# Four vector jobs moved in the steady step of a four-layer graph network

## The chip, the cores and the metric

The kernel runs on one core of one Trainium2 chip. The metric is device time in microseconds (us) of one execution. Times of runs are medians; the profile comes from one profiled execution of its own. The engines are named as in the profile: PE (TensorE matmuls), PEld (its weight loads), DVE (VectorE), ACT (ScalarE), POOL (GpSimd), SP (the queue that issues most transfers).

## What is computed

The input is x of 128 graphs x 64 nodes x 512 features, all float32, and a 64 x 64 matrix adj for each graph. Four layers follow each other; each adds its result to x and normalizes over the features. Cut to what matters:

```
H = (adj != 0);  Dn = 1 / (H @ adj[0]);  Be = 1 / column sums of H
conv(x, W, b) = Dn * (H @ (Be * (H.T @ (x @ W.T)))) + b
layer 0: h = layernorm(relu(conv(x, W1, b1))) * gamma + beta     # 512 -> 1024
         x = norm(x + conv(h, W2, b2) + x)                       # 1024 -> 512
layer 1: A = exp(leaky(8 * tanh((s_i + s_j) / 8))) * adj, rows normalized, times row sums of adj;  s = (x @ w) @ a
         x = norm(x + A @ x @ w)
layer 2: y = relu(adj @ (x @ W1) + b1); y = relu(adj @ (y @ W2) + b2)
         x = norm(x + adj @ (y @ W3) + b3)
layer 3: attention with 8 heads of 64; softmax(q k' / 8) * 0.33 + 0.33 * adj + 0.33 * exp(-adj), times v
         x = norm(x + heads @ W_out + b_out)
```

The mask that comes with the input is all true here; the kernel computes with it nonetheless.

## The kernel before

**Tiling.** Two graphs make a pair of 128 rows, four pairs a group (`G = 4`, 512 rows). The 128 graphs make 16 groups (`NGRP`), numbered q. `xg` holds a group's x and is changed in place by all layers.

**Products with weights.** Every product of a group with a 512 x 512 weight is a two by two block product with seven instead of eight block products (the scheme of Strassen and Winograd). The left side is a `Left`: its tile `aT_...` holds the transposed operand in four quadrants, and its method `sums` (lines 483 to 491) makes four sums of quadrants on DVE: s1, s2 and s4 in a tile `s_...`, s3 in place. The function `multiply` (line 514) issues the seven block products in the order B11, T1, T2, B21, T3, B22, T4, each through `product` (line 496). B11, T2, T3 and T4 go into one PSUM accumulator (`a_...`), T1 and B22 into a second (`b_...`), B21 into a third (`c_...`). Between them the accumulators are copied as they stand: u1 after B11, u5 after T1, u2 after T2 (function `snap`, line 521). With a residual the copy is an addition on DVE (line 526), without one it is a copy on ACT (line 524). T2 adds into the accumulator that u1 reads, so T2 has to wait for u1; T3 waits for u2 in the same way. Outputs are formed on DVE from an accumulator and a copy (lines 544, 548, 552), the last one on ACT or DVE (lines 555, 557). A block product is 8 passes of PE (16 in the product with W2, whose left side has two halves). In the profile a float32 matmul shows as two passes.

**Products with a graph's matrix** are 64 x 64 matmuls on quarters of PE (`graph_T`, line 448; profile names `gt_l`, `gt_l0h`, `gth`): 128 passes each, evacuated by ACT copies (line 466).

**Buffers.** PSUM has four accumulators (`ps_acc`) and four buffers for the small products (`ps_gt`). Weights come through a ring of 20 tiles (`RING`) by the SP queue, in the order of use.

**Order.** Three groups are in work at once: in a step, part `a` is layers 0 and 1 of group q, part `b` layer 2 and the first part of layer 3 of group q - 1, part `t` the end of layer 3 of group q - 2. Each is a generator (`first_half`, `second_half`) that stops at named points, and a list `order` (line 1205) written by hand says in which order the pieces are emitted; steps 2 to 15 are the steady ones. A scheduler then places each engine's instructions: among those that it reckons ready it takes the one that was emitted first. `tc.issue_after` holds instructions of an engine back until a named instruction of the same engine has been placed. The helper `behind(key)` (line 471) does this with an instruction that was put in the dictionary `last_add`. In the finished program each engine runs its list from front to back.

**Names around the change**, with the line where each stands:

- `left.sums()` of layer 2 (line 987), in `second_half`; its operand comes from `gt_l<-atc,x`.
- `doubled` and `constant` (lines 787 and 793): x becomes 2x + b2, and then x + cs * bw, where cs is a column scaling of the graph and bw a constant row. Both are emitted behind the last-but-one output of the first half block `l0w10` (lines 700 to 703).
- the eight sums of the two halves of the hidden layer (lines 723 and 724; names `s_l0h`, `aT_l0h`), between `c2a` and `c2b`.
- `gb3` (line 1002): four additions of a bias to x of group b; after it `prepare_masks` (lines 654 to 666; names `neg`, `m`, `adt`). Both stand behind the last-but-one output of the product `l2b`.
- `attend` (line 1172): the product of the probabilities with v, in two halves (duos) of two PSUM tiles each (`pv`), and the two scaled ACT copies of each duo into `aT_oT` (line 1195). The `osum` piece is the sums of that operand.

The end of the steady list, before the change:

```
    order = """
        t.v1 a.c1 t.v b.gt t.soft a.w1a1 a.w1a t.soft2 a.resid b.l2a1 b.l2a a.w1b1 t.ptp a.w1b t.pv a.lnh t.osum
        b.l2b1 a.c2a b.l2b a.c2b b.gb3 load a.w21 b.gh a.w2 rows b.l2c1 b.l2c2 a.ss b.l2c t.o1 a.den t.o2 a.c3 b.agg t.o
```

Of the kernel before, what the change touches and what calls it, by code (L numbers as in the profile page):

```python
# [8 lines left out]
FP = mybir.dt.float32  # L9
# [5 lines left out]
P = 128  # L15
# [7 lines left out]
Q = 256  # L23
# [18 lines left out]
def kernel(  # L42
# [31 lines left out]
    NGRP = NPAIR // G  # L74
# [6 lines left out]
    sp = ctx.enter_context(tc.tile_pool(name="sp", bufs=3))  # L81
# [54 lines left out]
    ten, vec, act = Engine(nc.tensor, PE), Engine(nc.vector, DVE), Engine(nc.scalar, ACT)  # L136
# [288 lines left out]
    def row2(t, c0):  # L425

        return t[:, c0 : c0 + Q].unsqueeze(1).to_broadcast([P, 2, Q])
# [38 lines left out]
            act.copy(o[:, :, :, g, :], ps[g])  # L466


    last_add = {}

    def behind(key):
        return tc.issue_after(last_add[key]) if key in last_add else nullcontext()

    class Left:
# [6 lines left out]
        def quad(self, m, k):  # L481
            return self.t[:, 2 * k : 2 * k + 2, m * Q : (m + 1) * Q]

        def sums(self):
            s = sp.tile([P, 3, 2, Q], FP, name=f"s_{self.key}", tag="s")
            s1, s2, s4 = (s[:, n] for n in range(3))
            s3 = self.quad(1, 0)
            vec.tensor_add(s1, s3, self.quad(1, 1))
            vec.tensor_sub(s2, s1, self.quad(0, 0))
            vec.tensor_sub(s3, self.quad(0, 0), s3)  # L490
            vec.tensor_sub(s4, self.quad(0, 1), s2)
            self.left = {
                B11: self.quad(0, 0), B21: self.quad(0, 1), B22: s4, T4: self.quad(1, 1),
                T1: s1, T2: s2, T3: s3,
            }
            return self
# [19 lines left out]
    def multiply(lefts, wt_q, dst, key, flipped=False, res=None, stops=(3,)):  # L516


        acc = [ps_acc.tile([P, 2, Q], FP, name=f"{n}_{key}", tag="acc") for n in "ab"]

        def snap(ps, m, n, what):
            t = work.tile([P, 2, Q], FP, name=f"{what}_{key}", tag="w")
            if res is None:
                act.copy(t, ps)
            else:
                vec.tensor_add(t, ps, res(m, n))  # L526
            return t

        pa, pc = acc
        product(pa, lefts, wt_q, B11, True, False, flipped)  # L530
        s1 = snap(pa, 0, 0, "u1")
        if 1 in stops:
            yield
        product(pc, lefts, wt_q, T1, True, False, flipped)
        s5 = snap(pc, 1, 1, "u5")
        if 2 in stops:
            yield
        product(pa, lefts, wt_q, T2, False, False, flipped)
        s2 = snap(pa, 0, 1, "u2")
        if 3 in stops:  # L540
            yield
        pb = ps_acc.tile([P, 2, Q], FP, name=f"c_{key}", tag="acc")
        product(pb, lefts, wt_q, B21, True, True, flipped)
        vec.tensor_add(dst(0, 0), pb, s1)
        if 4 in stops:
            yield
        product(pa, lefts, wt_q, T3, False, False, flipped)
        vec.tensor_add(dst(1, 1), pa, s5)  # L548
        if 5 in stops:
            yield  # L550
        product(pc, lefts, wt_q, B22, False, True, flipped)
        last_add[key] = vec.tensor_add(dst(0, 1), pc, s2).ins  # L552
        product(pa, lefts, wt_q, T4, False, True, flipped)
        if res is None:
            act.copy(dst(1, 0), pa)
        else:
            vec.tensor_add(dst(1, 0), pa, res(1, 0))
# [9 lines left out]
    def turned(t):  # L567

        return lambda m, n: t[:, 2 * n : 2 * n + 2, m * Q : (m + 1) * Q]
# [100 lines left out]
    def first_half(g):  # L670
        q, xg = g["q"], g["x"]
        pair = lambda p: xg[:, p, :]

        left = Left(f"l0_{q}")
# [5 lines left out]
        for n in range(2):  # L680
            for i, _ in enumerate(multiply(
                [left], (w_1[n], q),
                lambda m, k: h[m][:, :, n * D + k * Q : n * D + (k + 1) * Q],
                f"l0w1{n}_{q}",
                res=lambda m, k: row2(b1_bc, n * D + k * Q),
                stops=((2, 4), (2, 3))[n] if q == 1 else (3,),
            )):
                yield f"w1{'ab'[n]}{i + 1}"
            yield "w1" + "ab"[n]

            if n == 0:
                st = small.tile([P, G, 2, 6], FP, name=f"sth_{q}", tag="sth", bufs=2)
            with behind(f"l0w1{n}_{q}"):
                for m in range(2):
                    hn = h[m][:, :, n * D : (n + 1) * D]
                    act.activation(hn, hn, AF.Relu)  # L696
                    for p in range(2):
                        vec.bn_stats(st[:, 2 * m + p, n, :], hn[:, p, :])
            if n == 0:
                if q > 1:  # L700
                    with behind(f"l0w10_{q}"):
                        doubled(g)
                        constant(g)
                yield "resid"
        for m in range(2):
            mv = small.tile([P, 2, 2], FP, name=f"mvh_{q}_{m}", tag="mvh")
# [8 lines left out]
        lefts = [Left(f"l0h{u}_{q}") for u in range(2)]  # L715
        for duo in range(2):
# [3 lines left out]
                )  # L720
            if duo == 0:
                yield "c2a"
        for left in lefts:
            left.sums()
        yield "c2b"
        gen = multiply(lefts, (w_2, q), nat(xg), f"l0w2_{q}", res=nat(xg))
        next(gen)
# [4 lines left out]
        s4 = small.tile([P, G], FP, name=f"s4_{q}", tag="s4")  # L732
# [14 lines left out]
        t = grp.tile([P, G, C], FP, name=f"t_{q}", tag="t", bufs=1)  # L747
# [16 lines left out]
        left = Left(f"l1_{q}")  # L764
# [26 lines left out]
    def constant(g):  # L791
        for p in range(G):
            vec.scalar_tensor_tensor(
                g["x"][:, p, :], bw_bc, g["cs"][:, p : p + 1], g["x"][:, p, :], ALU.mult, ALU.add
            )
# [184 lines left out]
    def second_half(g):  # L980
        q, xg = g["q"], g["x"]
        pair = lambda p: xg[:, p, :]

        left = Left(f"l2_{q}")
        for duo in range(2):
            graph_T(pair, g["atc"], left.t, duo, f"l2_{q}")
        left.sums()
        yield "gt"
        h1 = Left(f"h1_{q}")
        for _ in multiply([left], (w_g[0], q), turned(h1.t), f"l2a_{q}", flipped=True):  # L990
            yield "l2a1"
# [5 lines left out]
        for _ in multiply([h1], (w_g[1], q), nat(g2), f"l2b_{q}"):  # L997
            yield "l2b1"
        yield "l2b"
        with behind(f"l2b_{q}"):  # L1000
            for p in range(G):
                vec.tensor_add(xg[:, p, :], xg[:, p, :], gb3_bc)
            prepare_masks(g)
# [4 lines left out]
        for c2 in range(2):  # L1008
            ps = [ps_gt.tile([P, 2, G, C], FP, name=f"gth2_{q}_{c2}_{h}", tag="gt") for h in range(2)]
            for c in range(2):  # L1010
                for p in range(G):
                    for f in range(2):
                        for h in range(2):
                            rows, c0 = slice(h * C, (h + 1) * C), (2 * c2 + c) * P + f * C
# [18 lines left out]
        for duo in range(2):  # L1033
            ps = [ps_gt.tile([P, D], FP, name=f"agg_{q}_{duo}_{p}", tag="gt") for p in range(2)]
            for h in range(2):
                for p in range(2):
                    rows = slice(p * C, (p + 1) * C)
# [11 lines left out]
        left = Left(f"xT_{q}")  # L1049

        for duo in range(2):
            ps = [ps_gt.tile([P, KD, 2, C], FP, name=f"xtp_{q}_{duo}_{h}", tag="gt") for h in range(2)]
            for c in range(KD):
                for p in range(2):
                    for h in range(2):
                        rows = slice(h * C, (h + 1) * C)
# [20 lines left out]
        v = big.tile([P, G, D], FP, name=f"v_{q}", tag="big")  # L1077
# [10 lines left out]
        pts = [turn_probs(g, duo, probs[duo]) for duo in range(2)]  # L1088
        yield "ptp"
        left = Left(f"oT_{q}")  # L1090
        for duo in range(2):
            attend(g, duo, pts[duo], v, left)
        yield "pv"
        left.sums()
        yield "osum"
        for n, _ in enumerate(multiply([left], (w_o, q), nat(xg), f"wo_{q}", res=nat(xg), stops=(1, 3))):
# [75 lines left out]
            pts.append(pt)  # L1172
        return pts

    def attend(g, duo, pts, v, left):

        q = g["q"]

        ps = [ps_acc.tile([P, 4, 2, C], FP, name=f"pv_{q}_{duo}_{gg}", tag="acc") for gg in range(2)]
        for hc in range(4):  # L1180
            for p in range(2):
                for h2 in range(2):
                    hd = 2 * hc + h2
                    for gg in range(2):
                        rows = slice(gg * C, (gg + 1) * C)
                        ten.matmul(
                            ps[gg][h2 * C : (h2 + 1) * C, hc, p, :],
                            v[rows, 2 * duo + p, hd * C : (hd + 1) * C],
                            pts[p][rows, h2 * 4 + hc, :],
                            start=True,  # L1190
                            stop=True,
                        )
        o4 = left.t[:, :, duo * Q : (duo + 1) * Q].rearrange("p c (a g i) -> p c a g i", a=2, g=2)
        for gg in range(2):
            act.mul(o4[:, :, :, gg, :], ps[gg], LA)  # L1195
# [7 lines left out]
        a0.c31 constant1 a1.w1a keep3 a1.resid a0.l12 a1.w1b1 a0.l13 a1.w1b2 b0.gt a1.w1b  # L1203
    """.split()
    order = """
        t.v1 a.c1 t.v b.gt t.soft a.w1a1 a.w1a t.soft2 a.resid b.l2a1 b.l2a a.w1b1 t.ptp a.w1b t.pv a.lnh t.osum
        b.l2b1 a.c2a b.l2b a.c2b b.gb3 load a.w21 b.gh a.w2 rows b.l2c1 b.l2c2 a.ss b.l2c t.o1 a.den t.o2 a.c3 b.agg t.o
        a.p1 b.xT a.p2 b.q1 b.q t.ln3 b.k1 prep b.k b.dots
    """.split()

# [5 lines left out]
    todo = []  # L1216
    for what in start:
        who, dot, name = what.partition(".")
# [7 lines left out]
    for step in range(1, NGRP + 2):  # L1226
        for what in order if step > 1 else step_1:
            who, dot, name = what.partition(".")
            key = (who, step - lag[who], name) if dot else (what, step + 1, None)
# [126 lines left out]
```

## Time and profile before

| | |
|---|---|
| median of 3 runs | 2805.87 us (2805.82 to 2807.02) |
| profiled execution | 2804.13 us |
| its span | 2802.3 us |
| PE busy | 2769.3 us, 99% of the span |
| PEld busy | 2362.0 us, 84% |
| DVE busy | 2003.7 us, 72% |
| ACT busy | 818.2 us, 29% |
| granted clock of PE, mean | 0.999 |
| a steady step | 171.8 us |

The span runs from the first to the last instruction; the profiled execution's own time is 1.8 us longer than its span. In the timeline each row gives the start in us from the span's start, the duration in us, the engine, the source line, the operation, the tiles (out<-in), the shapes, how many instructions were merged, and in brackets the idle time before the row with the instruction that ended it. A busy PE is not a PE at its peak, since matmuls overlap; the distance between the starts of two rows says more than the duration of a row. All times of single instructions given here are from one steady step, which begins about 1183 us into the span, and from the start of the next.

### The profile page before, as it was taken

The numbers are of one execution on the slowest core, as the hardware profiler recorded it, in microseconds if no ns is written. First come the engines' busy times: TensorE is split into PE (matmuls) and PEld (weight loads), VectorE is DVE, ScalarE is ACT, GpSimd is POOL, SyncE is SP. The second block draws the span as 40 slices with busy tenths as digits, with TensorE's granted clock in tenths as the row PEclk, the third lists the DMA queues.
The fourth block names the chain that finished last, engine by engine and source line by source line (L and its number), as shares of the span: only waits on it lengthen the run. The fifth ranks groups of instructions, "written<-read, shape, count | busy, mean of one in ns | idle before, by whom it ended". The sixth has DMA issues, their size and how long they took to land.

```text
span 2802.3 us, 67764 instructions
## 1 busy us (share of the span) xinstructions
PE 2769.3 (99%) x28862; PEld 2362.0 (84%) x28862; DVE 2003.7 (72%) x3861; ACT 818.2 (29%) x1467; POOL 38.1 (1%) x72
## 2 busy tenths in 40 slices
PE   9999999999999999999999999999999999999998
PEld 7878888888888888888888888888888888888877
DVE  6768677676776767767677776767767677676756
ACT  3223323232232322322233232232323223232222
POOL 2000000000000000000000000000000000000000
PEclk9999999999999999999999999999999999999999
DMA  8444454454544545445454454545545454454541
GB/s 259 165 127 148 130 158 140 139 162 131 165 129 136 163 129 166 127 142 163 133 158 130 142 160 128 162 129 150 152 133 162 130 158 135 132 162 129 147 118 64
DMA packets 309660, 405.94 MB, mean 145 GB/s; under 512 B 57424, under 2 KB 184944, under 8 KB 309360
## 3 DMA queue, kind: packets, MB, share of 16 engines
q1 hardware_dynamic: 304384, 385.84, 46.5%
q0 software_dynamic: 4976, 15.76, 1.5%
q8 instruction: 229, 3.75, 0.5%
q14 instruction: 71, 0.58, 0.1%
HBM read 370.57 MB, written 30.93 MB: 143 GB/s over the span
## 4 chain that ended last, share of the span: by engine, by line
PE 86%; DVE 8%; ACT 1%; issue 0%; DVEq 0%
PE a_l0w L509 13%; PE b_l0w L509 7%; PE a_l2b L509 4%; PE a_q L509 4%; PE a_k L509 4%; PE a_v L509 4%; PE c_l0w L509 4%; PE a_l2a L509 4%; PE a_l1w L509 4%; PE gt_l L458 3%; PE a_wo L509 3%; PE a_l2c L509 2%; PE gt_l0h L458 2%; PE b_l1w L509 2%; PE b_v L509 2%; PE b_l2b L509 2%
## 5 line engine op out<-in xcount | busy, mean ns | idle before, releaser
L509 PE MATMUL a_l0w<-w2w,aT_l0h 128*128 128x256 f32 x720 | 164.3, 381 | 0.0
L440 DVE BATCH_NORM_STATS2 st_l<-x 128x6 f32<-128x512 f32 x248 | 160.2, 674 | 0.1
L509 PEld LDWEIGHTS a_l0w<-w2w,aT_l0h 128*128 128x128 f32 x720 | 135.6, 190 | 18.8
L696 ACT ACTIVATE h<-h 128x1024 f32<-128x1024 f32 x58 | 61.3, 1057 | 216.6 <-DVE h L552 195.0
L444 DVE TENSOR_SCALAR x<-x,mv_l,rs_l 128x512 f32<-128x512 f32 x248 | 120.1, 542 | 1.8
L466 ACT COPY aT_l<-gt_l 128x512 f32<-128x512 f32 x176 | 90.5, 600 | 71.1 <-PE gt_l L458 71.0
L509 PE MATMUL b_l0w<-w2w,s_l0h 128*128 128x256 f32 x480 | 108.5, 379 | 0.0
L509 PEld LDWEIGHTS b_l0w<-w2w,s_l0h 128*128 128x128 f32 x480 | 90.1, 190 | 13.5
L1023 ACT ACTIVATE aT_h<-gth,gb_col 128x256 f32<-128x256 f32 x128 | 48.4, 489 | 159.0 <-PE gth L1015 159.0
L431 ACT ACTIVATE rs_l<-mv_l,eps_t 128x4 f32<-128x4 f32 (+1 forms) x63 | 18.8, 298 | 258.1 <-DVE mv_l L441 256.8
L509 PE MATMUL a_l2b<-gwbw,aT_h 128*128 128x256 f32 x360 | 86.9, 384 | 4.7 <-ACT aT_oT L1195 4.7
L509 PE MATMUL a_l2a<-aT_l,gwaw 128*128 128x256 f32 x360 | 86.6, 383 | 1.0 <-ACT aT_l L466 1.0
L509 PE MATMUL a_q<-aT_xT,wqw 128*128 128x256 f32 x360 | 86.6, 383 | 0.2 <-ACT aT_xT L1062 0.2
L509 PE MATMUL a_v<-wvw,aT_xT 128*128 128x256 f32 x360 | 86.6, 383 | 0.0
L509 PE MATMUL a_l2c<-gwcw,aT_h 128*128 128x256 f32 x360 | 85.3, 380 | 0.6 <-DVE g L548 0.6
L509 PE MATMUL a_wo<-wow,aT_oT 128*128 128x256 f32 x360 | 85.3, 380 | 0.0
L509 PE MATMUL a_l1w<-ww,aT_l 128*128 128x256 f32 x360 | 85.1, 379 | 0.0
L509 PE MATMUL a_k<-aT_xT,wkw 128*128 128x256 f32 x360 | 85.0, 379 | 0.0
L509 PE MATMUL a_l0w<-w1aw,aT_l 128*128 128x256 f32 x336 | 82.3, 388 | 0.0
L509 PE MATMUL a_l0w<-w1bw,aT_l 128*128 128x256 f32 x336 | 81.7, 379 | 0.0
L526 DVE TENSOR_TENSOR u_l0w<-a_l0w,b_bc 128x512 f32<-128x512 f32 x56 | 38.5, 688 | 59.8 <-PE a_l0w L509 59.8
L509 PEld LDWEIGHTS a_l2b<-gwbw,aT_h 128*128 128x128 f32 x360 | 67.1, 190 | 15.2 <-ACT aT_oT L1195 6.6
(503 smaller groups left out, 6464.5 us busy)
## 6 DMA issues: line engine op xcount, KB each, us to landing
w2w<-w2k SPq DMA_DIRECT2D x210, 256.0 KB, 2.7
x<-in_x_dram SPq DMA_DIRECT2D x15, 1024.0 KB, 6.3
w1aw<-w1ak SPq DMA_DIRECT2D x60, 256.0 KB, 2.7
w1bw<-w1bk SPq DMA_DIRECT2D x60, 256.0 KB, 2.7
ww<-wk SPq DMA_DIRECT2D x60, 256.0 KB, 2.7
gwaw<-gwak SPq DMA_DIRECT2D x60, 256.0 KB, 3.7
gwbw<-gwbk SPq DMA_DIRECT2D x60, 256.0 KB, 2.7
gwcw<-gwck SPq DMA_DIRECT2D x60, 256.0 KB, 2.7
```

The lines of the kernel that those rows point to most:

```text
L431: act.activation(rs[:, at], mv[:, at, 1], AF.Sqrt, bias=eps_t)
L440: vec.bn_stats(st, xg[:, p, :])
L444: vec.tensor_scalar(xg[:, p, :], xg[:, p, :], mv[:, p, 0:1], rs[:, p : p + 1], ALU.subtract, ALU.mult)
L458: ten.matmul(ps[g][f * C : (f + 1) * C, c, p, :], src(2 * duo + p)[rows, c0 : c0 + C], mat[rows, 2 * duo + p, :], start=True, stop=True,)
L466: act.copy(o[:, :, :, g, :], ps[g])
L509: ten.matmul(acc[:, blk, :], lhsT, rhs, start=(first and blk == 0 and i == 0), stop=(last and i == n_k - 1), skip_group_check=True,)
L526: vec.tensor_add(t, ps, res(m, n))
L696: act.activation(hn, hn, AF.Relu)
L1023: act.activation(o[:, :, h, :], ps[h][:, c].rearrange("p (d a) i -> p d (a i)", d=2), AF.Relu, bias=gb2_col[:, k : k + 1],)
```

## The change

Four things move; no arithmetic is added or removed.

1. `Left.sums` can make a part of its sums. In the steady steps the sums of layer 2 of group q are emitted behind the copy u2 of the next group's first half block (`l0w10`). The first and last group keep the old place.
2. `constant` moves from behind `l0w10` to behind the last-but-one output of `l2b`, ahead of the sums of the hidden layer; these sums are emitted quadrant sum by quadrant sum for both halves.
3. `gb3` and the masks move from behind that output of `l2b` to behind the last of the hidden layer's sums.
4. The ACT copies of the second duo of the value product are emitted behind u1 of `l2b`, and the sums of that operand after `b.l2b1`.

To make this possible, `snap` records its instructions in `last_add`. The core of the diff:

```diff
-        def sums(self):
-            s = sp.tile([P, 3, 2, Q], FP, name=f"s_{self.key}", tag="s")
-            s1, s2, s4 = (s[:, n] for n in range(3))
+        def sums(self, which=range(4)):
+            if 0 in which:
+                self.s = sp.tile([P, 3, 2, Q], FP, name=f"s_{self.key}", tag="s")
+            s1, s2, s4 = (self.s[:, n] for n in range(3))
             s3 = self.quad(1, 0)
-            vec.tensor_add(s1, s3, self.quad(1, 1))
-            vec.tensor_sub(s2, s1, self.quad(0, 0))
-            vec.tensor_sub(s3, self.quad(0, 0), s3)
-            vec.tensor_sub(s4, self.quad(0, 1), s2)
+            todo = (
+                lambda: vec.tensor_add(s1, s3, self.quad(1, 1)),
+                lambda: vec.tensor_sub(s2, s1, self.quad(0, 0)),
+                lambda: vec.tensor_sub(s3, self.quad(0, 0), s3),
+                lambda: vec.tensor_sub(s4, self.quad(0, 1), s2),
+            )
+            for n in which:
+                self.last = todo[n]().ins
...
         def snap(ps, m, n, what):
             t = work.tile([P, 2, Q], FP, name=f"{what}_{key}", tag="w")
-            if res is None:
-                act.copy(t, ps)
-            else:
-                vec.tensor_add(t, ps, res(m, n))
+            last_add[f"{key}.{what}"] = (act.copy(t, ps) if res is None else vec.tensor_add(t, ps, res(m, n))).ins
             return t
...
                 if q > 1:
                     with behind(f"l0w10_{q}"):
                         doubled(g)
-                        constant(g)
...
-        for left in lefts:
-            left.sums()
+        if q > 1:
+            with behind(f"l2b_{q - 1}"):
+                constant(g)
+        for n in range(4):
+            for left in lefts:
+                left.sums((n,))
+        last_add[f"l0h_{q}"] = lefts[-1].last
         yield "c2b"
...
-        left.sums()
+        alone = q == 0 or q == NGRP - 1
+        if alone:
+            left.sums()
         yield "gt"
+        if not alone:
+            with behind(f"l0w10_{q + 1}.u2"):
+                left.sums()
...
-        with behind(f"l2b_{q}"):
+        with behind(f"l0h_{q + 1}" if 0 < q < NGRP - 1 else f"l2b_{q}"):
             for p in range(G):
                 vec.tensor_add(xg[:, p, :], xg[:, p, :], gb3_bc)
             prepare_masks(g)
...
-        for duo in range(2):
-            attend(g, duo, pts[duo], v, left)
+        taken(0, attend(g, 0, pts[0], v), left)
+        ps = attend(g, 1, pts[1], v)
         yield "pv"
+        with behind(f"l2b_{q + 1}.u1"):
+            taken(1, ps, left)
         left.sums()
         yield "osum"
...
-        t.v1 a.c1 t.v b.gt t.soft a.w1a1 a.w1a t.soft2 a.resid b.l2a1 b.l2a a.w1b1 t.ptp a.w1b t.pv a.lnh t.osum
-        b.l2b1 a.c2a b.l2b a.c2b b.gb3 load a.w21 b.gh a.w2 rows b.l2c1 b.l2c2 a.ss b.l2c t.o1 a.den t.o2 a.c3 b.agg t.o
+        t.v1 a.c1 t.v b.gt t.soft a.w1a1 a.w1a t.soft2 a.resid b.l2a1 b.l2a a.w1b1 t.ptp a.w1b t.pv a.lnh b.l2b1
+        t.osum a.c2a b.l2b a.c2b b.gb3 load a.w21 b.gh a.w2 rows b.l2c1 b.l2c2 a.ss b.l2c t.o1 a.den t.o2 a.c3 b.agg t.o
```

`taken` holds the two ACT copies that stood at the end of `attend`, which now returns its PSUM tiles.

## The prediction

> **What bounds the kernel now.** I read the page's engine line first, then the waits of PE, then three stretches of the timeline inside one steady step.
>
> ```profile
> PE 2769.3 (99%) x28862; PEld 2362.0 (84%) x28862; DVE 2003.7 (72%) x3861; ACT 818.2 (29%) x1467; POOL 38.1 (1%) x72
> ```
>
> PE has work in 99% of the span. The chain of waits agrees (86% of the span is PE). One steady step, from the first second-layer product (line 509, `a_l0w<-w2w`) to the same product one step on, is 171.8 us (1183.46, 1355.24 us), and it comes again unchanged. So an edit is worth what it does to the PE order, and a wait put into PE is lost in full. The waits of PE:
>
> ```profile
> PE a_l2b L509 <- ACT aT_oT L1195: 4.7, 14, 0.3
> ```
>
> That 0.3 us per step is the only gap the view names, but small losses hide where PE changes tile shape or restarts. A steady product of 8 passes takes 1.727 us (1310.18, 1311.90, 1313.63); one of 16 takes 3.45; entering or leaving one from 64x64 work, or restarting after a wait, costs about 0.10 more (1281.03 to 1282.87). The timeline after the graph product of layer 2:
>
> ```profile
> 1300.78 0.68 DVE L491 TENSOR_TENSOR s_l<-aT_l,s_l 128x512 f32<-128x512 f32 x1
> ...
> 1301.12 1.03 PE L509 MATMUL c_l0w<-w1aw,aT_l 128*128 128x256 f32 x4
> 1301.38 0.69 DVE L526 TENSOR_TENSOR u_l0w<-a_l0w,b_bc 128x512 f32<-128x512 f32 x1
> 1302.12 1.59 PEld L509 LDWEIGHTS a_l0w<-w1aw,s_l 128*128 128x128 f32 x8 [0.37 <-DVE u_l0w L526]
> ```
>
> The four sums of layer 2 (lines 488 to 491) stand ahead of the copy u1 (line 526). T2 adds into the accumulator that u1 reads, so half of B21 (`c_l0w`) was put before it. The other stretch decides this case:
>
> ```profile
> 1352.20 2.49 DVE L1002 TENSOR_TENSOR x<-x,gb_bc 128x512 f32<-128x512 f32 x4
> 1354.42 2.05 ACT L466 COPY aT_l0h<-gt_l0h 128x512 f32<-128x512 f32 x4 [0.52 <-PE gt_l0h L458]
> 1354.60 0.42 DVE L654 TENSOR_TENSOR neg<-mj,mi 128x256 f32<-128x256 uint8 x1
> ...
> 1355.93 0.42 DVE L666 TENSOR_TENSOR adt<-adt,m 128x256 f32<-128x256 f32 x1
> 1356.27 0.69 DVE L488 TENSOR_TENSOR s_l0h<-aT_l0h 128x512 f32<-128x512 f32 x1
> ...
> 1358.79 3.62 PE L509 MATMUL b_l0w<-w2w,s_l0h 128*128 128x256 f32 x16
> ...
> 1361.34 0.69 DVE L526 TENSOR_TENSOR u_l0w<-a_l0w,x 128x512 f32<-128x512 f32 x1
> 1362.25 3.62 PE L509 MATMUL a_l0w<-w2w,s_l0h 128*128 128x256 f32 x16
> ```
>
> DVE runs without a pause from 1352.20: `gb3`, masks, eight sums, u1. u1 ends at 1362.03, and T2 (`a_l0w<-w2w,s_l0h`) starts at 1362.25. The slack is 0.2 us.
>
> [...] the DVE rows above follow the built order, and T2 waits at 1302.12 for a copy that itself stood behind the sums. [...] Here rows of 0.69 follow each other at 0.60, so I count start to start. [...] In the tail of this trace (2773 to 2777 us, PE busy 0.9 of 4 us) the granted clock then reads 0.50 for some 3.6 us.
>
> **The change part by part**, in the order that the built program has. Each item occurs in 14 steps.
>
> 1. Layer-2 sums behind u2 of `l0w10`. u1 then runs when B11 is done (about 1299.6, before T1 ends), and the built PE order has B21 whole. Now: T1 at 1299.40, B22 at 1306.72, which is 7.32 for four products; unbroken it is 4 x 1.727 = 6.91. **Gain 0.41.** The sums end at about 1306.8, and T1 of `l2a`, which reads them, comes near 1311: hidden. Next late: the read of T3 ends near 1307.5, T4 starts at 1308.0.
> 2. Scalings (`constant`, 4 x 0.66 = 2.65) leave their place at 1317.09, ahead of the `l2a` outputs. PE now puts 2 passes of `w1b` before T4 of `l2a`. From 1318.81 (B22) to 1324.20 is 5.39; unbroken 3 x 1.727 = 5.18. **Gain 0.21.**
> 3. Second copies of the value product (two ACT rows, 1.06 together at 1340.38) go behind u1 of `l2b`. u1 ran at 1341.52, and T2 waited for it until 1342.16 instead of 1342.00. From 1340.27 to 1344.08 is 3.81; unbroken 3.45 + 0.09 = 3.54. **Gain 0.27.** The 0.33 before `a_l2b` waits for the first copies, which do not move: no gain. The sums of oT move with the copies; the output product that reads them starts over 30 us later: nothing.
> 4. `gb3` and the masks go behind the last hidden sum, `constant` behind `l2b`'s last-but-one output, and the loop takes the sums quadrant by quadrant (the built DVE order still has left 0 whole, then left 1). On DVE: constant from 1352.20 to 1354.85. The first sum then waits for two ACT copies: 1354.42 + 0.49 + 0.58 = 1355.49. The eight sums take 5.07 (1356.27 to 1361.34), to 1360.57. `gb3` is emitted ahead of the product, and in the built order stands ahead of u1: 2.40 (1352.20 to 1354.60), to 1362.97. Four of five mask operations: 1.33 (1354.60 to 1355.93), to 1364.30. u1: 0.69, to 1364.99. T2 starts 0.05 later, as at 1302.12 behind u1's end of 1302.07: **1365.04 instead of 1362.25, 2.79 late.** Queued behind the waiting T2 on PE is everything else. The built order puts 17 of the 64 matmuls of `gth` ahead of it: 17/64 x 2.02 = 0.54 off; one more shape change costs 0.10. **Loss 2.35**, with PE idle some 2.1 (1362.25 + 0.08 + 0.54 to 1365.04).
> 5. The SP queue: four mask loads wait for `neg` and `m` (done near 1363.6, not 1355) and now stand among the weights of the output product. One `wo` weight behind them is issued some 2 us later than now, and is read more than 30 us after, with 2.7 us to land: nothing. Were that cover gone, it would cost that 2 us. The masks are read by the scores some 85 us later, x with `gb3` by `agg` 38 us later: nothing.
>
> Sum of a step: 2.35 - 0.41 - 0.21 - 0.27 = +1.46; 14 x 1.46 = **+20.4 us**. The profiled execution took 2804.13 us (span 2802.3 and 1.8 around it) and would be 2824.5; the median of 2805.87 stands 1.7 above it, so 2826.3, **2826**. Ends of the terms: the gains could be 0.4 (restarts stay) to 1.0, the loss 2.1 (mask operations at 0.34 each, copies sooner) to 2.6: 14 x 1.1 to 14 x 2.2, which is 2821 to 2837. A gain below nothing in 1 to 3 is not excluded, since T4 has 0.5 us of slack there.
>
> **Rivals.**
> - *u1 is not held* (faster). `gb3` and masks would fall into DVE's idle 2.76 us before the next copy (the wait ahead of 1365.90), and T2 start on time. Then 14 x -0.89 = -12.5, plus 14 x 0.2 for the split `gth`: about 2796. For it: DVE is busy only 72%, with room right after. Against it: the built order puts 8 operations ahead of u1[...]. It decides if the DVE block from constant to u1 is over 2.2 us shorter than summed.
> - *Half of the block hides* (within 0.2%). The loss falls to about 0.9 a step and cancels the gains: 2806. It needs the sums to start 1.4 us sooner, and the ACT copies forbid that.
> - *The idle 2.1 us drops the clock.* [...] If it drops each time, 3.4 us at half speed costs 1.7 a step, 14 x 1.7 = 24: about 2850; if in part, 2838. I take none and keep it for the range.
>
> **How the numbers follow.** Forecast (slower, 2820 to 2834) 0.79; clock drop 0.11; u1 not held 0.06; half hidden 0.04. About 0.2% (5.6 us) is what a measurement of this kernel tells from no change. Faster 0.06, within 0.2% 0.03, slower 0.91. For 8 in 10 I take 2817 to 2840, which takes in the term ends and part of the clock case.
>
> **What would show it.** In the profile after: a new row in the waits of PE, `a_l0w` (line 515 there) for DVE `u_l0w` (line 529), 14 times, near 2.1 us each; the steady step at 173.2; `c_l0w<-w1aw` in one piece of 8 passes; `gth` in pieces of 34 and 94 passes; the `gb_bc` rows starting 9.0 us after the row `g<-b_l2b` starts (now 0.6). Wrong if the step is shorter than 171.8, if T2 waits for a sum, a weight or a load instead, or if PEclk falls below 9.

## The result and the profile after

The changed kernel takes **2838.41 us** (median of four runs, 2835.98 to 2840.18), the kernel before 2806.36 (2805.82 to 2807.02, four runs). The ratio is 1.0113, with a 95% interval of 1.0099 to 1.0127: slower. The forecast was 2826 with a range of 2817 to 2840. The profiled execution took 2835.98 us with a span of 2834.2, which is 31.9 longer than the span before.

The page's engine line of the kernel after (busy time, share of the span, instructions):

```profile
PE 2774.8 (98%) x28862; PEld 2376.8 (84%) x28862; DVE 2005.6 (71%) x3861; ACT 816.6 (29%) x1467; POOL 38.1 (1%) x72
```

The counts of instructions are those of before; no work was added. PE is busy 5.5 us longer, so not all of the 31.9 us is a wait. The waits of PE, kernel after (total us, times, longest):

```profile
PE a_l0w L515 <- DVE u_l0w L529: 25.5, 14, 1.8
PE a_l2b L515 <- ACT aT_oT L1212: 4.7, 14, 0.3
```

The first row is new and is the forecast one: T2 of the W2 product waits for u1 in each of the 14 steady steps. The second row has not changed. The timeline of DVE, kernel after, shows what stands ahead of u1 (start, duration, operation, idle time before it in brackets):

```profile
1189.69 2.73 DVE L800 SCALAR_TENSOR_TENSOR x<-bw_bc,cs,x 128x512 f32<-128x512 f32 x4
1193.02 0.69 DVE L491 TENSOR_TENSOR s_l0h<-aT_l0h 128x512 f32<-128x512 f32 x1 [0.60 <-ACT aT_l0h L466]
...
1198.09 2.49 DVE L1014 TENSOR_TENSOR x<-x,gb_bc 128x512 f32<-128x512 f32 x4
1200.50 0.41 DVE L657 TENSOR_TENSOR neg<-mj,mi 128x256 f32<-128x256 uint8 x1
...
1201.71 0.68 DVE L529 TENSOR_TENSOR u_l0w<-a_l0w,x 128x512 f32<-128x512 f32 x1
```

The scalings run first and cost the chain nothing, since the first sum then waits 0.60 us for an ACT copy. The sums take 5.07 us from there, and behind them `gb3` and four mask operations stand ahead of u1, as the built order had it. PE in the same step:

```profile
1192.72 3.72 PE L515 MATMUL a_l0w<-w2w,aT_l0h 128*128 128x256 f32 x16
1196.28 3.62 PE L515 MATMUL b_l0w<-w2w,s_l0h 128*128 128x256 f32 x16
1199.83 0.79 PE L1027 MATMUL gth<-atc,g 64*64 64x64 f32 x34
1202.44 5.41 PE L515 MATMUL a_l0w<-w2w,s_l0h 128*128 128x256 f32 x16 [1.82 <-DVE u_l0w L529]
1207.78 1.62 PE L1027 MATMUL gth<-atc,g 64*64 64x64 f32 x94
1209.33 3.72 PE L515 MATMUL c_l0w<-w2w,aT_l0h 128*128 128x256 f32 x16
```

T2 starts 9.72 us after B11, where it was 7.01 before (1362.25 - 1355.24): 2.70 late. And this T2 takes 5.41 us for the same 16 passes that take 3.72 in the next step:

```profile
1377.33 3.72 PE L515 MATMUL a_l0w<-w2w,s_l0h 128*128 128x256 f32 x16 [1.82 <-DVE u_l0w L529]
```

Three windows of the trace of the kernel after, laid at the start and the end of the slow stretch, give the reason. The columns are the length of the window, the busy times of PE, PEld, DVE, ACT and POOL in it (with counts of instructions), then the granted clock, the DMA share and GB/s:

```profile
1199.24:1202.66 3.42, 1.59 (x39) 1.10 (x38) 3.42 (x10) 0.00 (x0) 0.00 (x0) 1.00 0.29 85
1202.66:1206.07 3.41, 3.41 (x9) 2.70 (x9) 0.66 (x2) 0.00 (x0) 0.00 (x0) 0.50 0.27 93
1206.07:1209.48 3.41, 3.41 (x103) 2.86 (x103) 0.69 (x1) 0.97 (x3) 0.00 (x0) 1.00 0.31 97
```

The wait itself falls at full clock; just behind it the clock reads 0.50 for 3.41 us, and then it is back. So the busy share of PE stays at 98% while the kernel loses time: work at half clock counts as busy. On the page the row of PEclk is 9 in all 40 slices, since a slice of 71 us averages 3.4 us at half clock away.

Where the 31.9 us of the span lie, worked out from the timeline. B21 starts 14.92 after B11 instead of 12.58, which is 2.34 in each of 14 steps: +32.8. The three gains take 0.90 from each step: -12.6. The clock halves in 5 of the 14 steps (those whose B11 starts at 844, 1192, 1540, 1888 and 2237), 1.69 each: +8.5. The remaining 3.2 occur once each: 1.2 ahead of the first W2 product, about 1.5 in one step (1.24 of it a wait of `gt_l` for which the trace names no releaser), about 0.7 behind the last steady step, where the trace has 6.83 us at half clock and that of before 3.41, and some tenths either way. A step in which the clock holds is 173.20 long.

### The profile page after: what moved, and what is told of

Its sections match the earlier page's. It is cut to its first block, busy times and chain, and to the rows that moved or that the text cites. A ratio compares the mean times of both kernels' runs of the same rounds, so it can differ in the third digit from the quotient of the medians.

```text
span 2834.2 us, 67707 instructions
## 1 busy us (share of the span) xinstructions
PE 2774.8 (98%) x28862; PEld 2376.8 (84%) x28862; DVE 2005.6 (71%) x3861; ACT 816.6 (29%) x1467; POOL 38.1 (1%) x72
## 4 chain that ended last, share of the span: by engine, by line
PE 81%; DVE 12%; issue 4%; ACT 2%; DMA 1%; POOL 0%; SPq 0%; DVEq 0%; POOLq 0%
PE a_l0w L515 11%; PE b_l0w L515 5%; PE a_q L515 4%; PE a_l2b L515 4%; PE a_k L515 4%; PE a_v L515 4%; PE c_l0w L515 4%; PE a_l1w L515 4%; PE a_l2a L515 4%; PE gt_l L458 3%; PE a_wo L515 3%; PE a_l2c L515 2%; PE b_l1w L515 2%; PE b_v L515 2%; PE b_l2b L515 2%
## 5 line engine op out<-in xcount | busy, mean ns | idle before, releaser
L515 PE MATMUL a_l0w<-w2w,s_l0h 128*128 128x256 f32 x240 | 64.1, 427 | 25.5 <-DVE u_l0w L529 25.5
L515 PEld LDWEIGHTS a_l0w<-w2w,s_l0h 128*128 128x128 f32 x240 | 50.3, 214 | 35.5 <-DVE u_l0w L529 27.4
```

Source lines behind the costliest of these rows:

```text
L515: ten.matmul(acc[:, blk, :], lhsT, rhs, start=(first and blk == 0 and i == 0), stop=(last and i == n_k - 1), skip_group_check=True,)
```

## The experiments

Kernels were compared with the kernel before on the same chip, at medians of 2805.4 (e1 to e4), 2805.69 (e5, e6, e8) and 2805.77 (e9). "B11 to T2" below is the distance of two starts in the timeline, 7.01 in the kernel before.

**Each gain by itself.** e3 has only the layer-2 sums of the change, e4 only the second copies, e2 both, without the moved scalings, `gb3` and masks. The core of e2 against the changed kernel:

```diff
-        if q > 1:
-            with behind(f"l2b_{q - 1}"):
-                constant(g)
-        for n in range(4):
-            for left in lefts:
-                left.sums((n,))
+        for left in lefts:
+            left.sums()
...
-        with behind(f"l0h_{q + 1}" if 0 < q < NGRP - 1 else f"l2b_{q}"):
+        with behind(f"l2b_{q}"):
```

(`constant(g)` stands behind `l0w10` again.) In e3 also the copies are as before, in e4 the layer-2 sums.

> The kernel before with the layer 2 sums alone moved behind u2 of the first half block. Theory A: 14 x 0.41 = 5.7 us less: 2800.7 us, step 171.4 us, the product B21 of the first half block in one piece of 8 passes. Rival C (the broken product cost nothing): 2806 us, step 171.8 us.

> The kernel before with only the second copies of the value product (and the sums behind them) moved behind u1 of l2b. Theory A: u1 of l2b is earlier, T2 of l2b no longer waits for it, 14 x 0.27 = 3.8 us less: 2802.6 us, step 171.5 us; the 0.33 us ahead of l2b's first product stays. Rival C (ACT is 29% busy, so where its copies stand does not matter): 2806 us.

> The changed kernel with the scalings, gb3, the masks and the order of the hidden sums put back as before; what is left is the moved layer 2 sums and the later second copies. Theory A: gains 0.41 + 0.27 a step, 14 x 0.68 = 9.5 us: 2797 us, step 171.1 us, no wait of T2. Rival B (these two moves cost): 2810 us or more. Rival C: 2806 us.

Measured: e3 2801.18 us, ratio 0.9985 [0.9979, 0.9992]; e4 2801.97, ratio 0.9988 [0.9982, 0.9995]; e2 2795.28, ratio 0.9965 [0.9953, 0.9978]. The steady step of 171.77 is 171.35 in e3 (0.42 less), 171.50 in e4 (0.27 less) and 171.08 in e2 (0.69 less, the sum of both). The gains are real, and in the steady step they add up. The whole times add up less well (4.2 and 3.4 us less in e3 and e4, 10.1 in e2): the profiled execution of e3 has three single steps that are 0.6 to 1.2 us longer than the steady one, and that of e4 has a half-clock stretch of its own near the end, outside the steady steps. In the changed kernel the gains show as products that follow each other unbroken:

```profile
1312.68 1.89 PE L515 MATMUL b_l0w<-w1aw,s_l 128*128 128x256 f32 x8
...
1316.13 1.89 PE L515 MATMUL c_l0w<-w1aw,aT_l 128*128 128x256 f32 x8
1317.86 1.89 PE L515 MATMUL a_l0w<-w1aw,aT_l 128*128 128x256 f32 x8
```

B21 (`c_l0w`) is in one piece, 1.73 from start to start, and T2 has no wait.

**The scalings back in their old place (e8).** Do they share in holding u1?

```diff
                     with behind(f"l0w10_{q}"):
                         doubled(g)
+                        constant(g)
...
-        if q > 1:
-            with behind(f"l2b_{q - 1}"):
-                constant(g)
```

> The changed kernel with only the scalings put back to their old place behind the first half block; gb3 and the masks stay ahead of u1. Theory A (the first hidden sum waits for the ACT copies anyhow, and gb3 and the masks hold u1): T2 still 2.7 us late, only the gain of 0.21 us a step is lost, step 173.4 us without a clock drop, 3 us more than the changed kernel: 2841 us, within 4 us for the number of drops. Rival B (2.65 us of scalings ahead of the sums are what holds u1): T2 starts nearly on time, 2800 us.

Measured: 2837.71 us, ratio 1.0112 [1.0096, 1.0129]. T2 stands at 9.71 behind B11 as in the changed kernel, the wait is 1.82 as there, and the step is 173.40 instead of 173.20. So the scalings take no part in the loss; moving them gains 0.20 a step. Five of 14 steps show half clock here too.

**`gb3` and masks out of the way (e1).** They are emitted behind the copy u2 of the W2 product instead of behind the last sum; all else is as in the changed kernel.

```diff
-        with behind(f"l0h_{q + 1}" if 0 < q < NGRP - 1 else f"l2b_{q}"):
+        with behind(f"l0w2_{q + 1}.u2" if 0 < q < NGRP - 1 else f"l2b_{q}"):
...
-        t.osum a.c2a b.l2b a.c2b b.gb3 load a.w21 b.gh a.w2 ...
+        t.osum a.c2a b.l2b a.c2b load a.w21 b.gb3 b.gh a.w2 ...
```

> The changed kernel with one thing different: the additions of gb3 and the masks stand behind the copy u2 of the W2 product instead of ahead of u1. Theory A (the nine operations ahead of u1 hold T2 and make the whole loss, and the clock drops come with that wait): the wait of a_l0w for DVE u_l0w is gone, the granted clock is back at 0.999, the three gains remain, 14 x 0.89 = 12.5 us less than before: 2794 us, steady step 170.9 us. Rival B (the loss comes from the scalings in front of the hidden sums, or from the later copies): still slower than before, 2820 us or more, and T2 still waits. Rival C (the gains are not there): 2806 us, step 171.8 us.

Measured: **2793.63 us** (2792.57 to 2795.96), ratio 0.9962 [0.9949, 0.9976]: faster than both kernels. T2 is at 7.01 again and a step 170.87 long, all 0.90 us of gain kept. The timeline of DVE in e1 shows the order that was needed:

```profile
1184.48 0.68 DVE L529 TENSOR_TENSOR u_l0w<-a_l0w,x 128x512 f32<-128x512 f32 x1
1186.32 0.69 DVE L529 TENSOR_TENSOR u_l0w<-b_l0w,x 128x512 f32<-128x512 f32 x1 [1.16 <-PE b_l0w L515]
1189.78 0.69 DVE L529 TENSOR_TENSOR u_l0w<-a_l0w,x 128x512 f32<-128x512 f32 x1 [2.76 <-PE a_l0w L515]
1190.39 2.49 DVE L1014 TENSOR_TENSOR x<-x,gb_bc 128x512 f32<-128x512 f32 x4
```

u1 runs at once behind the sums, and `gb3` starts behind u2. DVE is idle 2.76 us there, and the next operation behind the masks still waits 0.91 us for PE, so nothing is late next.

**Only the masks out of the way (e5).** `gb3` stays ahead of u1, `prepare_masks` goes behind u2.

```diff
                 vec.tensor_add(xg[:, p, :], xg[:, p, :], gb3_bc)
-            prepare_masks(g)
         yield "gb3"
+        with behind(f"l0w2_{q + 1}.u2" if 0 < q < NGRP - 1 else f"l2b_{q}"):
+            prepare_masks(g)
+        yield "masks"
```

> The changed kernel with only the masks moved behind u2 of the W2 product; gb3's four additions stay ahead of u1. Four mask operations fewer ahead of u1 take 1.33 us off its delay: T2 2.70 - 1.33 = 1.37 us late, no matmuls of gth ahead of it. [...] idle 1.4 us instead of 1.8 us is shorter, fewer drops, 0 to 2 of 14, none if the bound lies above 1.4 us; step 171.77 - 0.89 + 1.37 = 172.25 us, 14 x 0.48 = 6.7 us more than before: 2812 us. Rival (drops come with any wait of T2): some 5 drops of 1.7 us, 2820 us.

Measured: 2815.02 us, ratio 1.0032 [1.0020, 1.0044]. Waits and timeline of PE in e5:

```profile
PE a_l0w L515 <- DVE u_l0w L529: 18.7, 14, 1.3
```

```profile
1189.45 3.62 PE L515 MATMUL b_l0w<-w2w,s_l0h 128*128 128x256 f32 x16
1194.40 3.72 PE L515 MATMUL a_l0w<-w2w,s_l0h 128*128 128x256 f32 x16 [1.33 <-DVE u_l0w L529]
1198.05 2.09 PE L1029 MATMUL gth<-atc,g 64*64 64x64 f32 x128
```

T2 is 1.50 late and B21 1.60, since no part of `gth` runs ahead of T2 now and T2 takes 3.72 instead of 3.62 behind a wait. 14 x (1.60 - 0.90) = 9.8 over 2805.69 is 2815.5, which is what was measured. The size was expected some 3 us lower. More to the point: after a wait of 1.33 us **no** step shows half clock, and the mean clock is 0.999.

**A longer wait (e6).** Two more additions of 512 columns stand between `gb3` and the masks; their results are not used.

```diff
+            if 0 < q < NGRP - 1:
+                for n in range(2):
+                    spare = work.tile([P, D], FP, name=f"spare_{q}_{n}", tag="w")
+                    vec.tensor_add(spare, xg[:, n, :], gb3_bc)
             prepare_masks(g)
```

> The changed kernel with two more additions of 512 columns into a spare tile between gb3 and the masks (extra work, its result unused), 1.2 us more ahead of u1. T2 3.9 us late; 33 matmuls of gth instead of 17 stand ahead of it, so PE is idle some 2.5 us instead of 1.8 us and the next product starts 3.0 us late instead of 2.34. [...] 9 to 14 drops of 14 instead of 5. Sum: 14 x (3.04 - 0.89) = 30 us and 15 to 24 us of drops more than before, 2850 to 2860 us. Rival (drops at the same rate whatever the gap): about 5 drops, 2844 us.

Measured: 2843.22 us, ratio 1.0129 [1.0114, 1.0144]. The wait is 2.55 as wanted and T2 10.92 behind B11, but the number of halved steps was missed: five of 14 (the first four and the last), not nine or more, and the time is that of the rival (2844), not the 2850 to 2860 of the sum. In three of the five T2 is about 1.7 us longer, in two 3.0:

```profile
863.62 5.32 PE L515 MATMUL a_l0w<-w2w,s_l0h 128*128 128x256 f32 x16 [2.56 <-DVE u_l0w L529]
...
2604.98 6.73 PE L515 MATMUL a_l0w<-w2w,s_l0h 128*128 128x256 f32 x16 [2.56 <-DVE u_l0w L529]
```

So the length of the wait alone does not say whether the clock halves. Something else decides, and the place of the wait in time points to it. The traces show two things. A half-clock stretch in a steady step is 3.413 us long, or twice that; and in each of the three traces that have such steps the starts and ends of these stretches all lie on one grid of 3.4133 us, to within 1 ns. In the changed kernel the five stretches start at 854.50, 1202.66, 1550.82, 1898.98 and 2247.14, each 348.16 behind the one before, which is 102 x 3.4133. This grid cuts the execution into cells, and for each wait it can be read how much of PE's idle time falls into a single cell. The largest such part, in us:

```
changed kernel   half clock:  1.82 1.82 1.82 1.82 1.82
                 full clock:  1.82 1.49 1.44 1.35 1.29 1.26 1.23 1.15 1.03
e8               half clock:  1.82 1.82 1.82 1.82 1.82
                 full clock:  1.62 1.61 1.56 1.51 1.28 1.27 0.99 0.95 0.93
e6               half clock:  2.55 2.55 2.41 1.86 1.85
                 full clock:  1.71 1.59 1.56 1.45 1.43 1.41 1.40 1.30 1.29
```

So in these steps the clock halved, with one exception, when 1.82 us or more of the wait fell into one cell, which leaves PE busy for 47% of it or less, and a wait that an edge cuts into parts of 1.71 us or less was spared. Half clock began with the next cell (in the step shown above at 1202.66, with T2 started at 1202.44). In e5 (its grid taken from the stretch at the end of that kernel) the largest part is at most 1.34 us, and nine of its waits that lie whole in one cell are spared too. The exception is the wait at 2421.30 in the changed kernel, which lies whole in a cell, 0.09 us behind its edge, and is spared; why is open. Outside the steady steps the bound does not hold: the stretch near the end of e4 follows a cell with 1.35 us of idle time, most of whose work is 64 x 64.

The two T2 that lose 3.0 us are those with two half-clock stretches on end. Their waits are cut with 1.85 and 0.70 us on the two sides of the edge, and end inside the first slow cell. The windows of e6, columns as above:

```profile
2600.87:2604.28 3.41, 1.55 (x68) 1.12 (x66) 3.41 (x9) 1.57 (x4) 0.00 (x0) 1.00 0.55 154
2604.28:2607.69 3.41, 2.71 (x6) 2.18 (x7) 1.58 (x4) 0.00 (x0) 0.00 (x0) 0.50 0.00 0
2607.69:2611.11 3.42, 3.42 (x9) 2.70 (x8) 0.00 (x0) 0.00 (x0) 0.00 (x0) 0.50 0.00 0
2611.11:2614.52 3.41, 3.41 (x73) 2.83 (x72) 0.69 (x1) 1.56 (x4) 0.00 (x0) 1.00 0.59 155
```

The grid explains the nine spared steps of e6 as well: an undisturbed step there is 173.94 us, 51 cells less 0.14, so the wait hardly moves against the grid from step to step, and is hit or spared many steps running. The other executions of e6 fit that: one of the four took 2837.77 us at a mean clock of 0.998, beside 2846.48 at 0.994 in the profiled one. All this is read from the traces after the fact; no run was forecast from the grid.

**The wait filled with work (e9).** If idleness halves the clock and not the late T2 as such, then useless products in the gap must prevent it. In the changed kernel PE runs four more matmuls of the same shape (8 passes, as many as a block product has) between T1 and T2, into the accumulator that B21 overwrites afterwards; their result is not used. DVE keeps its order.

```diff
+        pb = None
+        if wt_q[0] is w_2 and wt_q[1] > 1:
+            pb = ps_acc.tile([P, 2, Q], FP, name=f"c_{key}", tag="acc")
+            for n in range(4):
+                ten.matmul(pb[:, 0, :], ones, wa_bc[:, 0:Q], start=True, stop=True)
...
-        pb = ps_acc.tile([P, 2, Q], FP, name=f"c_{key}", tag="acc")
+        if pb is None:
+            pb = ps_acc.tile([P, 2, Q], FP, name=f"c_{key}", tag="acc")
```

> The changed kernel with work added: between the first and the second copy of the W2 product, TensorE runs four more products of the same shape (8 passes, some 1.73 us) into the accumulator that the value product overwrites later; their result is thrown away. VectorE's order is untouched. Both theories: the second copy still starts 2.70 us late (9.71 us after the first), now with about 0.9 us of idle time ahead of it instead of 1.82, and all 64 gth products come after it; the steady step is 171.77 - 0.90 + 2.70 = 173.57 us where the clock holds. [...] no half-clock copies, granted clock 0.998 or more, 14 x 1.80 = 25 us over the kernel before: 2831 us, so faster than the changed kernel although it does more. Rival that the halved copies come with the late second copy itself and not with idleness: 5 to 7 of the 14 copies stay at 5.4 us, clock 0.995, about 2840 us.

Measured: 2833.67 us (2832.47 to 2836.31), ratio 1.0101 [1.0083, 1.0119], clock 0.999. Timeline of PE in e9:

```profile
1198.53 3.62 PE L515 MATMUL b_l0w<-w2w,s_l0h 128*128 128x256 f32 x16
1201.98 1.89 PE L545 MATMUL c_l0w<-wa_bc,ones 128*128 128x256 f32 x8
1204.68 3.72 PE L515 MATMUL a_l0w<-w2w,s_l0h 128*128 128x256 f32 x16 [0.81 <-DVE u_l0w L529]
1208.34 2.09 PE L1033 MATMUL gth<-atc,g 64*64 64x64 f32 x128
1210.36 3.72 PE L515 MATMUL c_l0w<-w2w,aT_l0h 128*128 128x256 f32 x16
```

T2 starts 9.71 behind B11, exactly as late as in the changed kernel, but none of the 14 is halved, though the starts of the waits lie all over a cycle of 3.413 us. So the late T2 as such does not halve the clock: with 0.81 us of idle time ahead of it the clock stayed up. In e5 and e9 the piece of `gth` ahead of the wait is gone too; that this piece is not needed for half clock shows in e6, where the halved wait at 508.52 stands in a cell with 2.55 us of idle time and 0.02 us of `gth`. B21 is 2.81 late (2.34 in the changed kernel, where a quarter of `gth` ran ahead of T2), so a step is 173.67, and 14 x (2.81 - 0.90) = 26.7 over 2805.77 gives 2832.5. The comparison of whole times is weaker than that of the traces: the median lies 4.7 us under that of the changed kernel, although 24 us of matmuls were added, but the two intervals overlap.

## Why the prediction was right, and where its size was off

- **What bounds the kernel**: right. PE has work nearly all the time, and what was put into its order was lost in full: 14 x 2.34 - 14 x 0.90 = 20.2 us, where the prediction had 20.4. The measured median lies above the 2837 to which the sum's own terms could stretch; it is inside the range because that took in part of the clock case.
- **Steps 1 to 3, the gains**: 0.41, 0.21 and 0.27 were predicted; 0.42 (e3), 0.20 (e8) and 0.27 (e4) were measured by themselves, 0.90 together (e1).
- **Step 4, the loss**: the chain on DVE came as summed. The first sum starts 0.30 behind B11 (predicted 0.25), the sums take 5.07, `gb3` 2.41 (2.40), the four mask operations 1.21 (1.33), and T2 follows the end of u1 by 0.05. T2 is 2.70 late instead of 2.79, B21 2.34 instead of 2.35, the idle time 1.82 instead of 2.1. e1 and e8 show whose work it was: `gb3` and masks, not the scalings. Of the difference of 0.35 in idle time (2.17 before rounding), 0.09 is the earlier T2; the rest is the piece of `gth` ahead of the wait, 34 passes as forecast, which lasts 0.79 and not 0.54. That B21 agrees so closely is in part luck: T2 came 0.09 sooner than summed, and the `gth` ahead of it saved 0.36 instead of 0.44.
- **Step 5, the SP queue**: no wait for a weight or a mask appears among the rows of PE that were not there before.
- **The rival of the unheld u1** fell for the reason given: the built order puts 8 operations ahead of u1, and u1 ran behind them in each of the 14 steps (in the step shown at 1201.71, though B11 had ended at 1196.44). e1 shows what it would have brought: its 2796 was 2793.63.
- **The rival of the clock** is the term that was mis-sized. The prediction worked it out rightly (1.7 a step when it drops, about 2838 if in part) and then put it at nothing in the sum ("I take none and keep it for the range"), at a chance of 0.11 that was the author's estimate. The 1.7 agrees with half of the 3.41 us for which the clock reads 0.50 in the tail of the trace of before (2777.00 to 2780.41; the prediction reads 3.6 there). The drop occurred in 5 of 14 steps of the profiled execution at 1.69 each, 8.5 us. That is most of the 11.5 by which this execution (2835.98) exceeds its predicted 2824.5; the other 3 are the items that occur once, and their cause is not settled. The fault lies in the reading of the tail: it showed a drop behind 4.00 us with PE busy for 0.89, which is 22%, and that no row showed a share between that and full work was taken for the absence of a drop. With the whole wait in one cell PE is busy for 47% of it (1.59 of 3.42 us in the window shown above), and that was enough in all but one case. The prediction's full price (a drop in each step, about 2850) was too high for a reason that it did not have: a wait is spared where an edge of the grid cuts it (in the changed kernel into parts of 1.49 us or less).
- **The signs named in advance**: the new row of waits, the step of 173.2, B21 in one piece, `gth` in 34 and 94 and the `gb_bc` rows 9.0 us behind the start of the row `g<-b_l2b` (1189.08 to 1198.09) all came. "PEclk below 9" never showed on the page and still half clock had cost 8.5 us: the sign was looked for in a view too coarse for it.

What stays open: the one-off items of some 3 us (e3, where T2 has no wait, has longer single steps too, so not all of them need come from the late T2); why one uncut wait was spared; how many half-clock stretches the three unprofiled runs of the changed kernel had (they took 2 to 4 us more than the profiled one, at mean clocks of 0.993 and 0.994 beside 0.995, which points to more of them, without a trace).

## What to carry to other kernels

Before moving vector work "to a quieter place", look up which copy the bounding engine waits for next and count everything that the move puts ahead of it in the same queue: here the four additions and the masks were 3.6 us ahead of a copy with 0.2 us of slack, and placing them behind the copy u2 turned a loss of 32 us into a gain of 12. When a forecast puts new idle time into TensorE, as here 1.82 us a step, price the clock with it: the wait was paid each time, and a half-clock stretch of 3.41 us behind it added 1.7 us in those steps of the loop in which the whole wait fell into one cell of the grid (5 of 14, with one such wait spared). Look for such stretches in the durations of equal products in the timeline, not in the busy share or in a page's clock row.

## What the runs showed of the hardware

- Behind a wait of 1.82 us, in a kernel in which PE has work in 98% of the span, the granted clock read 0.50 for 3.41 us in about a third of the cases (5 of 14, and 5 of 14 in e8); behind waits of 1.33 (e5) and 0.81 (e9) it never did in 14 cases each, and behind 2.55 us (e6) it did in 5 of 14.
- What told the halved waits from the spared ones in the steady steps is how much of a wait falls into one cell of a grid of 3.413 us, which is fixed within an execution and lies differently in each (its first edge is 1.16 us behind the start of the span in the changed kernel, 3.3 in e6): with 1.82 us or more the clock halved in 15 of 16 cases (changed kernel, e8, e6), with 1.71 or less in none of 54 (with e5 and e9). The longer wait of e6 was therefore not hit more often: its step of 173.94 us is near a multiple of the grid (51 x 3.413 = 174.08).
- A wait that reaches 0.70 us into the slow cell behind it brought a second one, 6.83 us at half clock in all (two cases in e6); T2 took 5.32 to 5.41 us with one slow cell and 6.73 with two, instead of 3.72.
- At full clock a product of 16 passes that restarted behind a wait, or followed 64 x 64 work, took 3.72 instead of 3.62 us (kernel after, e5, e9).
